# Moving gate rows to other engines and queues, and a weight preparation by one step, in a Mamba-style block on one core

## The chip, the cores and the metric

The kernel runs on one core of a Trainium2 chip. The metric is the device time of one execution in microseconds (us). A core has TensorE (PE; the profile lists its weight loads apart, as PEld), VectorE (DVE), ScalarE (ACT), GpSimd (POOL) and SyncE (SP), which here only issues DMAs. Each engine takes its own instructions strictly in the order of its queue; so does each engine's DMA issuing. A framework puts the instructions in order for every engine at build time, by the order of the program and by when it expects their inputs.

## The reference

For four sequences of 512 tokens with 512 features, the block computes

```python
mod = (silu(c) @ wmod).reshape(4, 6, 1, 512)      # sa, ca, ga, sb, cb, gb
ga = (2 * (ga >= 0) - 1) * maximum(abs(ga), 0.25) # gates; gb likewise
h = layernorm(x) * (1 + ca) + sa
x = x + ga * mamba2(h)                            # projection, conv, silu, chunked scan, output projection
h = layernorm(x) * (1 + cb) + sb
x = x + gb * (h @ binarized(weight).T + bias)
```

`binarized(w)` is the sign of each weight times the mean of the absolute values of its row. The Mamba part projects to x, B, C, z and dt, runs a causal convolution of four taps and SiLU over x, B and C, and then a scan in chunks of 128 tokens with 64 heads.

## The kernel before, in words

The 2,048 tokens are cut into eight halves of 256 tokens (`NHALF`, two to a sequence). Every half has two chunks, and every chunk four units of two head groups: 64 units in all. A unit takes one *step*. In a step `stage2` of unit s (the products `py`, L650, then gating by z) stands with `stage0` and `stage1` of unit s+2: `load_sums` (L535) fetches that unit's cumulated sums from DRAM (tile `decay`), `exps` (L544, line L549) takes 16 exponentials on ScalarE, and L625 multiplies them on VectorE by the masked product `gm`. The front part of half h+1 (norm, transposes `phT`, dt, projections and convolutions) is spread over the steps of half h by the list `SECOND` (`FRONT` for later halves); the tail of a chunk (`tail1`: the output projection `po`, L739, times the gates, L742; `tail2`: norm and transposes; `tail3`: the feed-forward product `pf`, L775) comes some steps after it. A table `steps`, filled by `at(step, f, ...)` from L814 on, holds all of this; within a step the functions are traced in the order in which they were entered.

What the change touches lies in steps 0 to 6, the first half's:

- `load_late` (step 0, L181) loads the modulation weights of the second, third, fourth and sixth part. They borrow tiles that are empty yet: `wout`, `bwT`, two z tiles and `room`, three rows of 512 per partition (L178), which later is the `gates` tile.
- `late_mods` (step 1, L233) multiplies them, copies the result to `rows` (L243; its tag `t` has one buffer, which the tail uses next), turns two of its parts into `modT`, and then makes the gate rows on the 64 partitions that hold them. VectorE does that in five instructions: twice the comparison with zero (L256), the absolute value as max(-g, g) (L257), the floor of 0.25 (L258), the product of sign and size (L259), and the second gate times the feed-forward bias `brow` (L260, 4 partitions). `brow` uses a buffer of tag `th`, `sg` and `ab` the two of tag `h2`. SyncE loads `brow` (L255) and writes the three rows to DRAM (`gate_d`, L262).
- `load_wout` (step 2, L265) loads the 2 MB output weights over the place of two modulation weights.
- `signs(o)` (steps 2 and 3, two of the four tiles each) loads a weight tile `fw` (L272, tag `h2`, two buffers, 256 KB), sums its absolute values (`alpha`, L274), makes its signs (`sw`, L277) and scales them on ScalarE (L278). `sw` lies in a buffer of tag `C` or `B`, three each, which also hold B and C of the halves.
- `turned_signs(o)` (steps 5 and 6) turns a tile on TensorE (L285) and copies it into `bwT` (L286), which `tail3` reads from step 7 on.
- `load_gates` (step 3, L719) broadcasts a sequence's rows from `gate_d` to all partitions; `tail1` reads them in step 4. `load_res` (L726) loads the residual `xr` in step 3.

`f_norm` of half 1 is also in step 1: statistics and L297 on VectorE, the root (`rs_a`, L298) on GpSimd, the normalisation (L300) on VectorE, then the transposes `phT` (L330). `f_dt` (step 2) is a chain of some 20 small VectorE instructions (L371 to L404), with four small DMA writes issued by GpSimd for all halves but the first (L389, L393, L407). A convolution (`conv_pair`, L440) starts on ScalarE (L450), takes three VectorE instructions (L454), which read the projection's PSUM tile, and ends with L459. PSUM tiles of tag `mm` have five buffers, and TensorE waits where the next product finds none.

Of the kernel before, what the change touches and what calls it, by code (L numbers as in the profile page):

```python
# [11 lines left out]
F32 = mybir.dt.float32  # L12
AF = mybir.ActivationFunctionType
ALU = mybir.AluOpType
# [4 lines left out]
B, L, DM = 4, 512, 512  # L19
# [21 lines left out]
def adaln_mamba_block(  # L41
# [15 lines left out]
    nc = tc.nc  # L57
# [13 lines left out]
    wk = ctx.enter_context(tc.tile_pool(name="wk", bufs=2))  # L71
# [47 lines left out]
    gate_d = dram.tile([B, 3, DM], F32, name="gate_d")  # L119
# [25 lines left out]
    def load_wm_at(t6, place, k0=0):  # L145

        n = place.shape[1]
        nc.sync.dma_start(place, wm_v[:, k0 : k0 + n, t6 * DM : (t6 + 1) * DM])
        for k in range(n):
            wms[t6, k0 + k] = place[:, k]  # L150
# [27 lines left out]
    room = wk.tile([P, 3, DM], F32, tag="gates", name="wm3_g", bufs=1)  # L178
    room_z = wm_tiles(3, "z", 6, 2)

    def load_late(h):  # L181

        load_wm_at(2, wout[:, 0:NK])
        load_wm_at(5, wout[:, NK:])
        load_wm_at(4, bwT)
        for k in range(2):
            load_wm_at(3, room_z[k].unsqueeze(1), k)
        load_wm_at(3, room[:, 0:2, :], 2)


    sc = keep.tile([P, NK, 32], F32, name="sc")
# [17 lines left out]
    def glued(products, after=None):  # L209

        with tc.issue_after(after) if after else nullcontext():
            first = products[0]()  # L212
        with tc.issue_after(first.ins), tc.high_priority(offset=1000):
            for product in products[1:]:
                product()  # L215
# [17 lines left out]
    def late_mods(h):  # L233

        pg = ps.tile([P, DM], F32, tag="mm", name="pg")
        glued([
            partial(
                mm, pg[32 * j : 32 * j + 32, :], sc[:, k, :], wms[t6, k], start=(k == 0), stop=(k == NK - 1)
            )
            for k in range(NK) for j, t6 in enumerate((2, 5, 4, 3))  # L240
        ])
        row = wk.tile([P, DM], F32, tag="t", name="rows", bufs=1)
        nc.vector.tensor_copy(row, pg)  # L243
        pm = ps.tile([P, NK, P], F32, tag="mm", name="pm")
        for dt in range(NK):
            nc.tensor.transpose(pm[:, dt, :], row[:, dt * P : (dt + 1) * P], ident)
        nc.vector.tensor_copy(modT[:, 2], pm[:, :, 96 : 96 + B])
        nc.vector.tensor_scalar(modT[:, 3], pm[:, :, 64 : 64 + B], 1.0, None, ALU.add)

        g = row[0:64, :]  # L250
        sg = wk.tile([64, DM], F32, tag="h2", name="sg")
        ab = wk.tile([64, DM], F32, tag="h2", name="ab")
        brow = wk.tile([64, DM], F32, tag="th", name="brow")
        second = slice(32, 32 + B)
        nc.sync.dma_start(brow[second, :], ffn_b.partition_broadcast(B))  # L255
        nc.vector.tensor_scalar(sg, g, 0.0, 2.0, ALU.is_ge, ALU.mult)  # L256
        nc.vector.scalar_tensor_tensor(ab, g, -1.0, g, ALU.mult, ALU.max)  # L257
        nc.vector.tensor_scalar(ab, ab, 0.25, None, ALU.max)  # L258
        nc.vector.scalar_tensor_tensor(sg, sg, -1.0, ab, ALU.add, ALU.mult)  # L259
        nc.vector.tensor_mul(ab[second, :], sg[second, :], brow[second, :])  # L260
        for i, v in enumerate((sg[0:B, :], sg[second, :], ab[second, :])):
            nc.sync.dma_start(gate_d[:, i, :], v)  # L262

    def load_wout():
        nc.sync.dma_start(wout, w_outT.rearrange("(k p) e -> p k e", p=P))  # L265
# [548 lines left out]
    def at(step, f, *args):  # L814
        steps.setdefault(step, []).append((f, args))

    for h in range(NHALF):
        for step, f, args in (FIRST, SECOND)[h] if h < 2 else FRONT:
            at(max(0, h - 1) * NU + step, f, h, *args)
        if h % HPB == 0:  # L820
            at(h * NU + 3, load_gates, h // HPB)
        if h == 0:
            at(0, load_late, h)
            at(1, behind, 0, late_mods)
            at(2, load_wout)
            for o in range(NK):
                at(o // 2 + 2, signs, o)
    for o in range(NK):
        at(o // 2 + 5, behind, 1, turned_signs, o)
    for h in range(NHALF):  # L830
# [9 lines left out]
    h = NHALF - 1  # L840
# [65 lines left out]
```

## Time and profile before

| | |
|---|---|
| median of three runs | 736.62 us (733.73 to 736.94) |
| the profiled execution's own time | 737.38 us |
| its span in the profile | 735.7 us |
| TensorE busy | 700.4 us (95%) |
| VectorE busy | 599.5 us (81%) |
| ScalarE busy | 522.0 us (71%) |
| GpSimd busy | 254.8 us (35%) |
| mean granted TensorE clock | 0.993 |

The profile is one execution. Its page cuts the span into 40 slices of 18.4 us and gives the busy share of each engine in tenths; PEclk is the clock that TensorE was granted, DMA the mean busy share of the 16 DMA engines. The chain of work that ended last is followed back from the last instruction, at each step to what released it. A line such as `PE a <- DVE b: 7.3, 2, 5.4` in the view of waits says that a on TensorE waited for b on VectorE 7.3 us in all, twice, at the longest 5.4. In the view of instructions over time a row has its start, its length (of several merged ones, from the first's start to the last's end), engine, line, operation, output and inputs, shapes and count, and in brackets how long the engine was idle before it and what ended that. SPq, DVEq and so on are the engines' queues, where DMAs are issued.

### The profile page before, as it was taken

How to read it: one execution, taken by the hardware profiler on the slowest of the kernel's cores; microseconds unless marked ns; L12 is line 12 of the kernel's file. 1: busy time of each engine (PE TensorE's matmuls, PEld its weight loads, DVE VectorE, ACT ScalarE, POOL GpSimd, SP SyncE). 2: the span in 40 equal slices, each digit the busy share in tenths (PEclk: the TensorE clock that was granted, in tenths of full speed). 3: DMA queues.
4: the chain of work that ended last, by engine and by line, in shares of the span. 5: the costliest groups of instructions: out<-in, count | busy, mean ns of one | idle time of the engine just before them, and what ended most of it. 6: DMA issues, size and time to landing. Idle time of an engine off the chain costs nothing.

```text
span 735.7 us, 15007 instructions
## 1 busy us (share of the span) xinstructions
PE 700.4 (95%) x5196; PEld 500.8 (68%) x5196; DVE 599.5 (81%) x1170; ACT 522.0 (71%) x1507; POOL 254.8 (35%) x297
## 2 busy tenths in 40 slices
PE   6999979899999999999999999999999999999997
PEld 3786746666677666677677666776667866677754
DVE  3869888876998678986899768996799867996995
ACT  2467658748696697785976787865968768788941
POOL 4021323444243332343223342433414332333652
PEclk9999989999999999999999999999999999999999
DMA  8991693535555256444644256552564537457720
GB/s 279 328 291 41 204 208 85 135 98 142 127 132 144 63 155 137 102 115 102 159 116 130 53 116 168 142 137 53 140 132 114 130 86 176 116 150 151 142 69 29
DMA packets 119067, 99.24 MB, mean 135 GB/s; under 512 B 73984, under 2 KB 97152, under 8 KB 118992
## 3 DMA queue, kind: packets, MB, share of 16 engines
q1 hardware_dynamic: 117808, 96.39, 52.3%
q0 software_dynamic: 896, 1.38, 0.7%
q8 instruction: 41, 0.67, 0.4%
q10 hardware_dynamic: 288, 0.52, 0.2%
q14 instruction: 34, 0.28, 0.1%
HBM read 92.47 MB, written 5.79 MB: 134 GB/s over the span
## 4 chain that ended last, share of the span: by engine, by line
PE 65%; ACT 16%; DVE 9%; DMA 4%; issue 4%; POOL 1%; SPq 1%; ACTq 0%; DVEq 0%; POOLq 0%
PE po L739 14%; PE pp_x L434 11%; PE pp_z L434 10%; ACT decay L549 9%; PE pp_C L434 7%; PE pp_B L434 5%; PE pf L775 3%; PE py L212 2%; PE py L215 2%; DVE decay L625 2%; ACT h L759 2%; DVE u_x L454 2%; DMA fw<-in_ffn_w 2%; ACT win L549 2%; PE gy L215 2%
## 5 line engine op out<-in xcount | busy, mean ns | idle before, releaser
L549 ACT ACTIVATE decay<-decay,st 128x128 f32<-128x128 f32 x960 | 293.9, 395 | 4.2 <-DMA decay<-sums_d 3.7
L625 DVE SCALAR_TENSOR_TENSOR decay<-decay,gm 128x1024 f32<-128x1024 f32 x120 | 160.8, 1341 | 50.3 <-ACT decay L549 47.2
L434 PE MATMUL pp_x<-hT,win 128*128 128x259 f32 x512 | 120.7, 390 | 7.3 <-DVE u_C L454 7.3
L434 PE MATMUL pp_z<-hT,win 128*128 128x256 f32 x512 | 118.1, 383 | 0.0
L434 PEld LDWEIGHTS pp_x<-hT,win 128*128 128x128 f32 x512 | 96.9, 193 | 25.2 <-ACT decay L549 7.7
L739 PE MATMUL po<-wout,z 128*128 128x512 f32 x256 | 113.8, 595 | 0.0
L434 PEld LDWEIGHTS pp_z<-hT,win 128*128 128x128 f32 x512 | 94.3, 189 | 16.3 <-issue 3.5
L675 POOL TENSOR_TENSOR z<-yt,z 128x256 f32<-128x256 f32 x62 | 62.9, 1015 | 76.1 <-DVE yt L674 57.8
L454 DVE SCALAR_TENSOR_TENSOR u_x<-pp_x,cw,u_x 128x256 f32<-128x256 f32 x192 | 83.6, 474 | 1.3 <-ACT u_x L450 0.7
L739 PEld LDWEIGHTS po<-wout,z 128*128 128x128 f32 x256 | 47.5, 190 | 53.1 <-issue 52.4
L672 POOL TENSOR_TENSOR yt<-yt,xs 128x256 f32<-128x256 f32 x46 | 41.4, 899 | 106.3 <-DVE yt L671 78.6
L507 POOL TENSOR_TENSOR xs<-u_x,rr 128x512 f32<-128x512 f32 x32 | 42.7, 1334 | 79.2 <-DVE u_x L459 61.3
L516 ACT ACTIVATE uz<-pp_z,zb 128x256 f32<-128x256 f32 x64 | 27.5, 470 | 59.0 <-PE pp_z L434 59.0
L215 PE MATMUL py<-decay,xpad 128*32 128x128 f32 x1680 | 66.3, 276 | 0.0
L434 PE MATMUL pp_B<-hT,win 128*128 128x259 f32 x256 | 63.5, 396 | 2.7 <-ACT decay L549 1.9
L434 PE MATMUL pp_C<-hT,win 128*128 128x259 f32 x256 | 59.6, 384 | 1.1 <-DVE u_x L454 1.1
L775 PE MATMUL pf<-bwT,h 128*128 128x512 f32 (+1 forms) x136 | 59.0, 578 | 1.4 <-ACT h L759 1.3
L434 PEld LDWEIGHTS pp_B<-hT,win 128*128 128x128 f32 x256 | 47.4, 193 | 14.5 <-ACT decay L549 3.1
L450 ACT ACTIVATE u_x<-pp_x,cb,cw 128x256 f32<-128x256 f32 x64 | 35.3, 560 | 30.5 <-PE pp_x L434 30.4
L434 PEld LDWEIGHTS pp_C<-hT,win 128*128 128x128 f32 x256 | 47.8, 189 | 9.4 <-PE pn L424 1.4
L679 POOL TENSOR_TENSOR xd<-xpad,st 128x256 f32<-128x256 f32 x48 | 34.1, 727 | 55.8 <-PE pst L215 28.3
L212 PE MATMUL py<-decay,xpad 128*32 128x128 f32 x240 | 47.4, 279 | 3.2 <-issue 2.2
(157 smaller groups left out, 1080.9 us busy)
## 6 DMA issues: line engine op xcount, KB each, us to landing
decay<-sums_d SPq DMA_DIRECT2D x120, 256.0 KB
decay<-sums_d SPq DMA_DIRECT2D x120, 128.0 KB
rr<-r_d SPq DMA_DIRECT2D x64, 128.0 KB
e<-e_d SPq DMA_DIRECT2D x96, 64.0 KB
win<-in_w_inT SPq DMA_DIRECT2D x4, 1024.0 KB
xr<-in_x SPq DMA_DIRECT2D x16, 256.0 KB
res<-o SPq DMA_DIRECT2D x15, 256.0 KB
x<-in_x SPq DMA_DIRECT2D x14, 256.0 KB
```

What stands on the lines that cost most here:

```text
L212: first = products[0]()
L215: product()
L434: last = mm(pm, win[:, k, col : col + P], H[h]["hT"][:, k, lo:], start=(k == 0), stop=(k == NK - 1))
L450: nc.scalar.activation(u[:, j, :], pm[:, KS - 1 :], AF.Identity, bias=cb[:, t : t + 1], scale=cw[:, t, KS - 1 : KS])
L454: nc.vector.scalar_tensor_tensor(u[:, j, :], pm[:, k : k + T], cw[:, t, k : k + 1], u[:, j, :], ALU.mult, ALU.add)
L507: nc.gpsimd.tensor_tensor(xs, xc, rr, ALU.mult)
L549: nc.scalar.activation(ets[r][:, i, :], ets[r][:, i, :], AF.Exp, bias=H[h]["st"][:, hd : hd + 1], scale=-1.0)
L625: nc.vector.scalar_tensor_tensor(ets[r], ets[r], 1.0, bc_mid(gm[:, r, :], HPG), ALU.min, ALU.mult)
L672: ew.tensor_add(t, t, xs)
L675: ew.tensor_mul(zg, t, zg)
L739: last_po = mm(po, H[h]["z"][g // 2][:, g % 2, c * CH : (c + 1) * CH], wout[:, g, :], start=(g == 0), stop=(g == NKI - 1))
L775: mm(pf, h2[:, k, :], bwT[:, k, cols], start=(k == 0), stop=(k == NK - 1))
```

## The change

The gate rows leave `late_mods` for a function `late_gates`, called in step 2 after `load_wout`. The comparison stays on VectorE (now giving plus or minus one half), the absolute value goes to ScalarE, the floor (now with a doubling) and the two products go to GpSimd, and the three writes of `gate_d` go to GpSimd's queue. `sg`, `ab` and `brow` lie in the three rows of `room`, not in buffers of `h2` and `th`; `brow` is loaded at the end of `load_late`, in step 0. `signs` comes one step later for every tile (steps 3 and 4); `turned_signs` stays in steps 5 and 6.

```diff
@@ load_late
         load_wm_at(3, room[:, 0:2, :], 2)
+        nc.sync.dma_start(brow[second, :], ffn_b.partition_broadcast(B))
@@ late_mods
-        g = row[0:64, :]
-        sg = wk.tile([64, DM], F32, tag="h2", name="sg")
-        ab = wk.tile([64, DM], F32, tag="h2", name="ab")
-        brow = wk.tile([64, DM], F32, tag="th", name="brow")
-        second = slice(32, 32 + B)
-        nc.sync.dma_start(brow[second, :], ffn_b.partition_broadcast(B))
-        nc.vector.tensor_scalar(sg, g, 0.0, 2.0, ALU.is_ge, ALU.mult)
-        nc.vector.scalar_tensor_tensor(ab, g, -1.0, g, ALU.mult, ALU.max)
-        nc.vector.tensor_scalar(ab, ab, 0.25, None, ALU.max)
-        nc.vector.scalar_tensor_tensor(sg, sg, -1.0, ab, ALU.add, ALU.mult)
-        nc.vector.tensor_mul(ab[second, :], sg[second, :], brow[second, :])
+        late_row.append(row)
+
+    late_row = []
+    second = slice(32, 32 + B)
+    brow = room[0:64, 2, :]
+
+    def late_gates(h):
+        g = late_row.pop()[0:64, :]
+        sg, ab = room[0:64, 0, :], room[0:64, 1, :]
+        nc.vector.tensor_scalar(sg, g, 0.0, 0.5, ALU.is_ge, ALU.subtract)
+        nc.scalar.activation(ab, g, AF.Abs)
+        nc.gpsimd.tensor_scalar(ab, ab, 0.25, 2.0, ALU.max, ALU.mult)
+        nc.gpsimd.tensor_tensor(sg, sg, ab, ALU.mult)
+        nc.gpsimd.tensor_tensor(ab[second, :], sg[second, :], brow[second, :], ALU.mult)
         for i, v in enumerate((sg[0:B, :], sg[second, :], ab[second, :])):
-            nc.sync.dma_start(gate_d[:, i, :], v)
+            nc.gpsimd.dma_start(gate_d[:, i, :], v)
@@ the table of steps
             at(2, load_wout)
+            at(2, late_gates, h)
             for o in range(NK):
-                at(o // 2 + 2, signs, o)
+                at(o // 2 + 3, signs, o)
```

## The prediction, made before the result was known

> **What bounds the kernel now.** I read the page's slices first: TensorE is 95% busy, and one slice is unlike the rest.
>
> ```profile
> PE   6999979899999999999999999999999999999997
> ...
> PEclk9999989999999999999999999999999999999999
> DMA  8991693535555256444644256552564537457720
> ```
>
> In the sixth slice (92 to 110 us) the clock that TensorE was granted falls, and before it DMA goes from empty to full. The waits between 64 and 150 us show TensorE's longest one there (total, times, longest):
>
> ```profile
> PE pp_x L434 <- DVE u_C L454: 7.3, 2, 5.4
> ```
>
> Stages of 3 us around it (columns: length, then PE, PEld, DVE, ACT, POOL busy with counts, clock, DMA share, GB/s):
>
> ```profile
> 91.00:94.00 3.00, 2.88 (x46) 1.99 (x44) 2.64 (x9) 1.58 (x4) 2.79 (x6) 1.00 1.16 198
> 94.00:97.00 3.00, 0.05 (x2) 0.00 (x0) 1.56 (x3) 1.09 (x2) 1.18 (x2) 1.00 1.09 230
> 97.00:100.00 3.00, 0.59 (x2) 0.53 (x3) 3.00 (x9) 2.48 (x8) 0.00 (x0) 0.61 1.03 279
> 100.00:103.00 3.00, 3.00 (x9) 2.33 (x8) 3.00 (x7) 1.10 (x3) 0.00 (x0) 0.50 1.07 260
> 103.00:106.00 3.00, 3.00 (x15) 2.33 (x13) 1.52 (x5) 2.71 (x9) 1.34 (x2) 0.75 1.05 181
> ```
>
> TensorE stands still for 5.4 us and then runs 6 us at a half to three quarters of its clock. The chain of that stretch (start, length, what) says why:
>
> ```profile
> 76.64 1.00 DVE ab L260
> ...
> 77.66 0.24 SPq L262
> ...
> 82.26 0.76 SPq L272
> ...
> 83.06 13.38 DMA fw<-in_ffn_w
> ...
> 96.46 0.69 DVE alpha L274
> ...
> 98.08 1.19 DVE u_C L454 x3
> ...
> 99.41 6.23 PE pp_x L434 x16
> ```
>
> The last gate row on VectorE (L260) holds SyncE's queue; behind it queue `wout` (2 MB) and the first two `fw` tiles; `fw` takes 13.38 us to land because DMA is full; VectorE's queue stands at `alpha` (L274), and the convolution of C, which must empty the PSUM tile that the next `pp_x` needs, is behind it. SyncE's own waits, and VectorE's queue:
>
> ```profile
> SPq L255 <- DVE u_x L459: 10.9, 1, 10.9
> ...
> SPq L262 <- DVE sg L259: 4.8, 1, 4.8
> SPq L262 <- DVE ab L260: 3.7, 1, 3.7
> ```
>
> ```profile
> 95.13 0.69 DVE L274 TENSOR_REDUCE alpha<-fw 128x1 f32<-128x512 f32 x1 [1.49 <-DMA fw<-in_ffn_w]
> 95.73 0.42 DVE L277 TENSOR_SCALAR sw<-fw 128x512 f32<-128x512 f32 x1
> 96.46 0.69 DVE L274 TENSOR_REDUCE alpha<-fw 128x1 f32<-128x512 f32 x1 [0.32 <-DMA fw<-in_ffn_w]
> 97.07 0.42 DVE L277 TENSOR_SCALAR sw<-fw 128x512 f32<-128x512 f32 x1
> ```
>
> SyncE stood 10.9 us before `brow` and 8.5 us before the gate rows' writes while DMA was nearly idle (share 0.07 from 64 to 76 us). After 125 us no single wait of TensorE is over 2.2 us, so what is won here stays won unless steps 3 to 6 give it back.
>
> **The change, part by part.** The sum is made against the profiled execution (737.38 us: span 735.7 and 1.7 around it); the median shown is 736.62, 0.8 less.
>
> *Gate rows off VectorE.* Removed: L256 0.42, L257 0.68, L258 0.41, L259 0.67, L260 0.99, start to start some 2.9 us. One comparison of L256's form returns (0.42). L256 to L258 stand right before `rs_a` (L297, 71.13), whose root on GpSimd releases the normalised x and so the transposes `phT`, before which TensorE waits 0.24 and 1.01 us. With `rs_a` some 1.3 us earlier those waits go; next late is TensorE itself, whose `pp_z` runs to 74.67. **-1.2 us.**
>
> *ScalarE's Abs.* It is between 0.27 (Abs 128x128, L372) and 0.59 us (copy 128x512, L223); I take 0.59, whose row has the same 512 columns. ScalarE idles 3.21 us before 74.71, which hides it; uncovered it would cost 0.59. L372 stands beside exponentials, and the trace has one table load in all, so none is added.
>
> *GpSimd's three operations and three DMA issues.* A product with 512 columns takes 1.28 (L745); two make 2.56. A one-input operation of this form isn't in the trace: between a 64x512 memset (0.66, L317) and the product (1.28); I take 1.0. The issues cost 0.53 to 0.77 each (L407, L393), 1.7 for three; a write lands after 1.8 to 1.9. In all 5.3 us of GpSimd, which idles 8.0 us before 85.10 and 4.0 before 90.66: hidden. Behind the gate rows on that queue stand the xs product and half 1's four DMA issues (90.66); if the 8.0 us gap weren't used, those would be up to 5.3 late, and what they write is read only some 25 us later. What it costs is VectorE's speed beside GpSimd: L459 takes 0.69 alone and 1.22 beside GpSimd's L675. Three GpSimd operations slow between none and three such instructions: 0 to +1.6; I take **+0.4**, as VectorE then runs mostly the short chain of f_dt.
>
> [...]
>
> *SyncE's queue.* `brow` moves to step 0, where its place in `room` is free. Gone are the 10.9 us before `brow` and the 4.8 and 3.7 before the gate writes. Behind them stood the third unit's decay sums, `rr`, `wout` and `fw`. `wout` waits for the last read of `wm2` and `wm5` (68.7) and can go about 10 us earlier, into idle DMA. Alone this is worth between 0 and 1.5 us (the third unit's exponentials come earlier, with ScalarE idle anyway); I take 0, but it makes the next term safer. The added wait: load_gates now follows GpSimd's writes. Behind it on SyncE stand `fw`, the residual `xr` and the fifth unit's sums; today it is issued at 95.12, and the writes should have landed near 88.
>
> *Signs one step later.* `alpha` and `sw` for o = 0, 1 leave the place before C's convolution. VectorE then goes from 93.6 straight to it; of the 5.36 us TensorE still waits for two or three convolution instructions, 0.9: **-4.5**. The first `pp_x` after it takes 6.23 us where others take 3.51 to 3.77: with the clock kept, **-2.5**. Intervals of 1 to 2 us elsewhere (before `phT`, for one) show no lower clock.
>
> [...]
>
> Given back: the four moved instructions (2.0 us start to start) land in 97 to 113, from which o = 2, 3's two reductions (1.27) go one step on. VectorE is busy 15.6 us from 94 to 113.8 today, 3.5 of them signs; with the new ones (2.2) that makes 14.3. From 92.4 (93.6 less the first term) it ends at 106.7, while TensorE, 8.2 earlier, would end `po` (113.8) at 105.6. That bounds the loss at 1.1 above and 0 below (VectorE idles 3 us there today); **+1.1**. In the next step VectorE sets the end (t, xr, the norm, 113.8 to 121.8), and two reductions are added: **+1.2**. `fw` shares buffers only with h2 now, so o = 0, 1 wait for no gate row; o = 2, 3 wait for their sw as before. The turning stays in steps 5 and 6, TensorE's work is the same. The sw tiles hold their B and C buffers one step less.
>
> Sum: -1.2 + 0.4 - 4.5 - 2.5 + 1.1 + 1.2 = **-5.5 us**: 731.9 against the profiled run, **731.1** against the median. Bounds: all gains, nothing back and the queue's 1.5: -9.7; gains halved and all given back: about 0.
>
> **Rivals.**
> 1. *The stall moves.* `alpha` waits for `fw` again, one step later, now in front of the tail's t and xr. For it: `fw` still queues behind load_gates and sums on SyncE, and a tile took 13.38 us to land. Against: `wout`, the bulk of the queue, should be gone. Then terms 2 and 3 come back as 7.0 elsewhere: -5.5 + 7.0 = +1.5, less up to 1.5 from the earlier sums: about 737.
> 2. *SyncE stands at load_gates.* If GpSimd takes the gate rows only behind f_dt's four issues, z and xd (to 95.2 today), they are written at 95.2 + 5.3 + 1.9 = 102.4, 7.3 us after today's 95.1. `fw`, xr and the fifth unit's sums then leave 7.3 late, VectorE stands at `alpha` in front of the tail, and the clock falls again (2.5): -5.5 + 7.3 + 2.5 = +4.3, **740.9**. It decides once the writes land more than some 4 us after SyncE gets there. Against it: the 8 us gap on GpSimd, and inputs ready at 69.7.
> 3. *The order is what counts and TensorE is full anyway:* the 5.4 us go, but VectorE, 87% busy from 64 to 150 us (75.1 of 86), gives nearly all back in steps 4 to 6; what stays is the 0.8 to 2.5 us by which its own work shrinks (2.9 less 0.4, less up to 1.7 for GpSimd): 734 to 736.
>
> **How the numbers follow.** My forecast (727 to 733) has 0.60; rivals 1 and 3 together 0.23; rival 2 0.17. Under 0.5% (3.7 us) a measurement can't tell from no change: faster 0.60, same 0.23, slower 0.17. The range takes in the bound below (727) and reaches through rivals 1 and 3 into rival 2's nearer half: 727 to 739.5. The forecast's own range is 727 to 733.
>
> **What would show it.** Right: SyncE issues `wout` near 70 us; no wait of TensorE over 2 us from 85 to 125; the granted clock stays at 1.0; the `pp_x` that took 6.23 takes under 4; load_gates waits little. Wrong: a wait of VectorE on `fw` before `alpha` in step 3 or 4 (rival 1); a long wait of SyncE on gate_d (rival 2); VectorE gapless to 150 us with TensorE waiting in small pieces (rival 3). The prediction fails altogether if the framework, which orders each engine's queue, reshuffles what comes after 125 us, which I take as unchanged.

## The result and the profile after

The changed kernel took **743.09 us** in the median of five runs (741.36 to 744.98), the kernel before 736.05 on the same chip: a ratio of 1.0105 (interval 1.0075 to 1.0135), 7 us slower where 5.5 us faster was forecast. The profiled execution's span is 741.4 us against 735.7, so the trace holds 5.7 us of the loss. Behind the change's own lines the line numbers are 9 higher than before (L434 is L443, L549 is L558). Units are counted from one here; the expectations for e1 to e5 count from zero where they call the unit with the exponentials around `hT` the third: it is the fourth.

From the page of the kernel after, the slices of TensorE's clock:

```profile
PEclk9999989899999999999999999999999999999999
```

The clock now falls twice, in the sixth slice as before (mean granted clock 0.82 from 92 to 111 us, before and after) and in the eighth (0.81 from 130 to 148 us). TensorE's waits from 60 to 160 us (total, times, longest):

```profile
PE pp_x L443 <- DVE u_C L463: 5.5, 1, 5.5
PE pp_x L443 <- ACT xpad L502: 4.4, 1, 4.4
PE pa L377 <- ACT hT L356: 2.5, 2, 1.3
```

The stall near 97 us, which was to go, is still there (5.36 before, 5.55 now). There is a new one of 4.4 us on ScalarE's copy `xpad`, and one of 2.5 us on `hT`. The starts of TensorE's products say where the time was lost: the first `po` starts 0.6 us earlier (106.62, now 106.02) but takes 7.72 us instead of 7.13 while the clock is still low (0.69 from 106 to 108 us, 1.00 before), and so ends level (113.75 and 113.74); the `pp_x` behind the new stall starts 4.3 us later (132.44, now 136.78); `pf` is 5.7 later (141.34, now 147.01), and so is everything after it. The whole loss thus arises between 114 and 147 us; the gains and losses ahead of it cancel. About 1.9 us of it are there before the new stall, in small waits of TensorE (the `py` in front of the stall starts at 129.43 before and at 131.31 now); the stall and the lower clock behind it (0.55 from 136 to 142 us) make the rest. The new stall in TensorE's queue:

```profile
136.78 6.01 PE L443 MATMUL pp_x<-hT,win 128*128 128x259 f32 x16 [4.38 <-ACT xpad L502]
```

The two stalls have different histories. The first, in VectorE's queue of the kernel after:

```profile
97.45 0.47 DVE L463 SCALAR_TENSOR_TENSOR u_C<-pp_C,cw,u_C 128x256 f32<-128x256 f32 x1
97.85 1.21 DVE L634 SCALAR_TENSOR_TENSOR decay<-decay,gm 128x1024 f32<-128x1024 f32 x1
98.98 0.67 DVE L283 TENSOR_REDUCE alpha<-fw 128x1 f32<-128x512 f32 x1
99.57 0.41 DVE L286 TENSOR_SCALAR sw<-fw 128x512 f32<-128x512 f32 x1
99.91 0.67 DVE L283 TENSOR_REDUCE alpha<-fw 128x1 f32<-128x512 f32 x1
100.50 0.41 DVE L286 TENSOR_SCALAR sw<-fw 128x512 f32<-128x512 f32 x1
100.83 0.47 DVE L463 SCALAR_TENSOR_TENSOR u_C<-pp_C,cw,u_C 128x256 f32<-128x256 f32 x1
```

`alpha` and `sw` of o = 0, 1, entered one step later, stand in front of the last instruction of C's convolution; before, they stood in front of its last four. The fifth unit's two decay products (L634, at 95.11 and 97.85) now stand in front of it too; before, they came behind it (101.53 and 106.22). No row has an idle time: VectorE waits for no `fw` any more, it is simply full from 94 to 106. The second stall is prepared on ScalarE. Busy time in stages of 6 us (the fourth pair of columns is ScalarE), first of before, then of after:

```profile
111.00:117.00 6.00, 6.00 (x47) 3.73 (x46) 4.48 (x9) 4.76 (x13) 0.00 (x0) 1.00 0.08 17
117.00:123.00 6.00, 5.22 (x63) 4.09 (x61) 5.58 (x10) 6.00 (x19) 4.11 (x4) 1.00 0.34 96
```

```profile
111.00:117.00 6.00, 6.00 (x61) 3.82 (x60) 3.96 (x9) 1.35 (x2) 0.00 (x0) 1.00 0.02 9
117.00:123.00 6.00, 4.84 (x56) 4.03 (x54) 4.61 (x11) 1.90 (x4) 4.50 (x5) 1.00 0.61 144
```

ScalarE worked 10.76 of these 12 us before, and 3.25 now. The first copy `xpad` in its queue before, and its queue after:

```profile
130.48 0.59 ACT L493 COPY xpad<-pt_xt 128x512 f32<-128x512 f32 x1
```

```profile
116.02 0.72 ACT L287 ACTIVATE sw<-sw,alpha 128x512 f32<-128x512 f32 x1 [4.26 <-DVE sw L286]
...
120.52 0.40 ACT L558 ACTIVATE decay<-decay,st 128x128 f32<-128x128 f32 x1
123.19 0.72 ACT L287 ACTIVATE sw<-sw,alpha 128x512 f32<-128x512 f32 x1 [2.27 <-DVE sw L286]
...
130.57 2.45 ACT L558 ACTIVATE decay<-decay,st 128x128 f32<-128x128 f32 x8
132.91 0.56 ACT L459 ACTIVATE u_C<-pp_C,cb,cw 128x256 f32<-128x256 f32 x1
133.35 2.45 ACT L558 ACTIVATE decay<-decay,st 128x128 f32<-128x128 f32 x8
135.69 0.56 ACT L459 ACTIVATE u_C<-pp_C,cb,cw 128x256 f32<-128x256 f32 x1
136.14 0.58 ACT L502 COPY xpad<-pt_xt 128x512 f32<-128x512 f32 x1
```

It idles, or waits for `sw`, and then the seventh and eighth units' exponentials stand in one block with the copies of C (`u_C`, 127.24 before, 132.91 now) and `xpad` (130.48 before, 136.14 now). TensorE waits for that copy. Why it idled: the sixth unit's exponentials, which ran at 112 to 118 before, now run at 102 to 108, as their sums come earlier; and the seventh's can't be had, since their tile is read by the fifth unit's `py`. Before, half of that `py` stood ahead of `po` in TensorE's queue (106.05); now all of it stands behind (114.75). The first rows of that `py`, before and after, and the row of SyncE's queue after that fetches those sums:

```profile
106.05 0.30 PE L212 MATMUL py<-decay,xpad 128*32 128x128 f32 x1
```

```profile
114.75 0.30 PE L213 MATMUL py<-decay,xpad 128*32 128x128 f32 x1
```

```profile
115.50 0.49 SPq L550 DMA_DIRECT2D decay<-sums_d  x1
```

### The profile page after: what moved, and what is told of

Read it like the earlier page. It is cut to its first block, busy times and chain, and to the rows that moved or that the text cites. A ratio compares the mean times of both kernels' runs of the same rounds, so it can differ in the third digit from the quotient of the medians.

```text
span 741.4 us, 15011 instructions
## 1 busy us (share of the span) xinstructions
PE 701.7 (95%) x5196; PEld 501.8 (68%) x5196; DVE 596.0 (80%) x1166; ACT 522.6 (70%) x1508; POOL 259.7 (35%) x303
## 4 chain that ended last, share of the span: by engine, by line
PE 61%; ACT 19%; DVE 12%; issue 4%; DMA 2%; POOL 1%; SPq 0%; ACTq 0%; POOLq 0%; DVEq 0%
PE po L748 13%; ACT decay L558 11%; PE pp_x L443 11%; PE pp_z L443 10%; PE pp_C L443 6%; PE pp_B L443 5%; PE pf L784 3%; DVE decay L634 3%; DVE u_x L463 2%; PE py L216 2%; PE py L213 2%; ACT h L768 2%; ACT win L558 2%; DMA decay<-sums_d 2%; PE gy L216 1%
## 5 line engine op out<-in xcount | busy, mean ns | idle before, releaser
L558 ACT ACTIVATE decay<-decay,st 128x128 f32<-128x128 f32 x960 | 294.0, 395 | 2.8 <-DMA decay<-sums_d 2.6
L634 DVE SCALAR_TENSOR_TENSOR decay<-decay,gm 128x1024 f32<-128x1024 f32 x120 | 160.9, 1342 | 55.0 <-ACT decay L558 53.1
L443 PE MATMUL pp_x<-hT,win 128*128 128x259 f32 x512 | 122.4, 394 | 9.9 <-DVE u_C L463 5.5
L443 PE MATMUL pp_z<-hT,win 128*128 128x256 f32 x512 | 118.1, 383 | 0.0
L443 PEld LDWEIGHTS pp_x<-hT,win 128*128 128x128 f32 x512 | 97.8, 195 | 28.1 <-issue 8.1
L443 PEld LDWEIGHTS pp_z<-hT,win 128*128 128x128 f32 x512 | 94.4, 189 | 16.2 <-issue 3.5
L443 PE MATMUL pp_B<-hT,win 128*128 128x259 f32 x256 | 62.6, 391 | 2.7 <-ACT decay L558 1.9
L443 PE MATMUL pp_C<-hT,win 128*128 128x259 f32 x256 | 59.6, 384 | 1.2 <-DVE u_x L463 1.2
L443 PEld LDWEIGHTS pp_B<-hT,win 128*128 128x128 f32 x256 | 46.5, 189 | 14.1 <-ACT decay L558 3.1
L443 PEld LDWEIGHTS pp_C<-hT,win 128*128 128x128 f32 x256 | 47.9, 190 | 9.1 <-PE pn L433 1.4
L688 POOL TENSOR_TENSOR xd<-xpad,st 128x256 f32<-128x256 f32 x48 | 35.1, 747 | 46.5 <-ACT xpad L502 24.9
```

The source lines that it names most:

```text
L443: last = mm(pm, win[:, k, col : col + P], H[h]["hT"][:, k, lo:], start=(k == 0), stop=(k == NK - 1))
L558: nc.scalar.activation(ets[r][:, i, :], ets[r][:, i, :], AF.Exp, bias=H[h]["st"][:, hd : hd + 1], scale=-1.0)
L634: nc.vector.scalar_tensor_tensor(ets[r], ets[r], 1.0, bc_mid(gm[:, r, :], HPG), ALU.min, ALU.mult)
```

## The experiments

Every kernel was timed against the kernel before on the same chip. The theories, in the order in which they were formed: T1, the later signs cost, by the C buffer that `sw` of o = 2 waits for; T2, the front costs, by Abs and by exponentials ahead of `hT`; T3, freeing SyncE's queue costs, by early sums; T4, the place of the fifth unit's `py` costs.

**e1 and e2: the two parts alone.** e1 has the gate rows' part, with `signs` in their old steps; e2 has only the later `signs`.

```diff
# e1, against the kernel after
-                at(o // 2 + 3, signs, o)
+                at(o // 2 + 2, signs, o)
# e2, against the kernel before
-                at(o // 2 + 2, signs, o)
+                at(o // 2 + 3, signs, o)
```

> The gate rows' part of the change alone; the signs stay in steps 2 and 3. Theory T1 (the loss comes from the signs' step: the sw tile of o = 2 gets its C buffer only when o = 0 has been turned in step 5, ScalarE stands before its scaling, and 16 exponentials behind it come late, so that TensorE stands 4.4 us near 132 us and loses its clock): this kernel lacks that stall and is 5 to 8 us faster than the changed kernel, 734 to 738. Theory T2 (the loss comes from the front: Abs stands on ScalarE's queue 2.7 us before the exponentials, and the third unit's exponentials, whose sums now come early, go between the four hT copies, so that the chain of f_dt starts 3.2 us late): it is as slow as the changed kernel, 741 to 744.

> The signs one step later alone; the gate rows stay on VectorE and SyncE's queue. T1: it has the stall near 132 us and loses 4 to 7 us against the kernel before, 740 to 743. T2: it is as fast as before or faster, and, with the alpha reductions gone from before C's convolution, TensorE's wait of 5.4 us near 94 us shrinks: 729 to 736.

e1: 740.82 us, ratio 1.0062 (1.0048 to 1.0076). e2: 732.65, ratio 0.9961 (0.9948 to 0.9974). The signs' part does what the prediction said in kind, at some two thirds of the size (-4.7 forecast, some -3 measured); the gate rows' part, which was put at -0.8 us, costs 4 to 5. Neither reproduces the stall of 4.4 us on `xpad`. Of the 6.8 us that e1's view puts on exponentials, 4.0 are the old stall's place (98.81) and 2.8 lie before the second `pp_x` (141.24); in both places an instruction of the convolution on VectorE ended within 0.1 us of the exponential, so which of the two released TensorE isn't told apart. The parts don't add: +0.62% and -0.39% make +0.23%, and the whole is +1.05%. TensorE's waits from 60 to 160 us, e1 and then e2:

```profile
PE pp_x L443 <- ACT decay L558: 6.8, 2, 4.0
```

```profile
PE pp_x L434 <- DVE u_C L454: 3.4, 2, 1.9
```

**e3 and e4: the turning earlier, and Abs on VectorE.** Both against the whole change.

```diff
# e3
-        at(o // 2 + 5, behind, 1, turned_signs, o)
+        at(o // 2 + 4, behind, 1, turned_signs, o)
# e4
-        nc.scalar.activation(ab, g, AF.Abs)
+        nc.vector.scalar_tensor_tensor(ab, g, -1.0, g, ALU.mult, ALU.max)
```

> The changed kernel with the turning also one step apart as before (steps 4 and 5 in place of 5 and 6), so that o = 0's buffer is free a step earlier. T1: the wait of ScalarE before the scaling of o = 2 goes, and with it the stall near 132 us: 735 to 738. T2: nothing changes in the front, 741 to 744.

> The changed kernel with the absolute value on VectorE (one instruction of 0.68 us, as before) and not on ScalarE. T1: within 1.5 us of the changed kernel, 741 to 744. T2: the 2.7 us before the exponentials go, hT and f_dt come 2 to 3 us earlier, and the time falls by 2 to 3, to 739 to 741.

e3: 736.36, ratio 1.0002 (0.9989 to 1.0014); the stall near 132 is gone, that near 97 stays at 5.5. e4: 743.83, ratio 1.0109 (1.0094 to 1.0124). Abs on ScalarE isn't the cause. e3 seemed to show that the C buffer, which keeps `sw` of o = 2 waiting until o = 0 is turned, is; but in its trace half of the fifth unit's `py` is ahead of `po` again (108.00, `po` 108.79), so it changed two things.

**e5 to e8: the front, and SyncE's queue alone.**

```diff
# e5, against e1; e7 has it too
-  (2, f_hT, ()), (2, f_dt, ()),
+  (1, f_hT, ()), (2, f_dt, ()),
# e6, against the kernel before; the added line ends load_late
+        nc.sync.dma_start(room[32 : 32 + B, 2, :], ffn_b.partition_broadcast(B))
-        brow = wk.tile([64, DM], F32, tag="th", name="brow")
+        brow = room[0:64, 2, :]
-        nc.sync.dma_start(brow[second, :], ffn_b.partition_broadcast(B))
# e7, against the kernel after: e3 and e5 together
# e8, against e2: e3's line
```

> The gate rows' part alone (as in e1: signs at their old steps), with f_hT of half 1 entered one step earlier, so that its copies of hT stand on ScalarE ahead of the third unit's 16 exponentials again. In e1 TensorE waited 2.5 us for hT, and the part alone cost 4.6 us (740.8 against 736.2). T3 (with SyncE's queue freed, the decay sums come early and exponentials stand on ScalarE in front of the copies that TensorE needs): the wait on hT is under 0.5 us, the chain of f_dt starts some 2.5 to 3 us earlier than in e1, and the time is 737 to 739; the rest of e1's loss, the waits of pp_x on the exponentials near 130 us (1.5 and 2.8), stays unless it follows from the front. Rival (the order in front is harmless, the loss is made near 130 us alone): the wait on hT goes, and the time stays at 740 to 741.5.

> The kernel before with one edit: the 4-partition load of brow goes to step 0 and to the third row of room; the gate rows stay on VectorE and on SyncE's queue, signs in their old steps. No compute instruction is added, removed or moved by the program; only SyncE's wait of 10.9 us ahead of brow goes, so that what is queued behind it comes earlier. T3: the earlier sums put exponentials ahead of copies on ScalarE, so the kernel becomes slower, by 1.5 to 4.5 us: 737.5 to 740.5. The rival, which is the prediction's own figure for SyncE's queue (0, at best -1.5): 734.5 to 736.2.

> The whole change, with the turning one step earlier (as in e3, 736.4) and f_hT of half 1 one step earlier (as in e5): both places where the runs so far show a wait that the change brought are undone. T3: TensorE's 2.5 us for hT go, the chain of f_dt and with it the convolution of C starts 2 to 3 us earlier, so the 5.5 us wait of pp_x for u_C near 97 us falls to 2 to 3 us, and with it the clock's fall: 731 to 734. Rival (VectorE is gapless from 94 us on and sets the end of that stage whatever comes ahead of it): 735.5 to 737.

> The kernel before with the signs one step later (as in e2, 732.7) and the turning one step earlier; gate rows as before. If the buffers of C that the signs hold cost time in e2 as they did in the whole change, this gives another 1 to 3 us: 730 to 731.5. If they only cost time where ScalarE's queue is filled with early exponentials (T3), there is nothing to win here: 732 to 734, TensorE's work of turning being only moved.

e5: 740.09, ratio 1.0063 (1.0043 to 1.0083). The wait on `hT` is gone and the ratio is e1's, as the rival said. Its profiled run doesn't show that what is won in front is lost again: there `po` starts 1.6 us before e1's (104.22, e1 105.83) and the span is 1.4 us shorter (737.6, e1 739.0), but the six runs spread from 738.8 to 743.6. e6: 735.44, ratio 1.0 (0.9991 to 1.0009). The sixth unit's exponentials come at 104.8, as in the slow kernels, and nothing is lost. But e6 frees SyncE's queue only in part. The wait before `brow` moves to the gate rows' writes, which VectorE still feeds (13.4 us there, 4.8 before); the third unit's sums are fetched at 73.00 (73.35 before, 63.42 in the whole change) and `wout` is issued at 77.36 (81.79 and 68.40). So T3 falls for what e6 frees; the whole freeing wasn't timed apart from the rest of the gate rows' part. e7: 733.19, ratio 0.9965 (0.9951 to 0.9979), the change itself with two edits, and faster than both kernels. e8: 736.08, ratio 0.9998 (0.9985 to 1.0011): the edit that wins 7 us in e3 loses 3 in e2, since the turning now stands ahead of `po` and TensorE waits there for `sw` (1.8 us in all), after a wait of `py` for exponentials (1.8, at 100.70).

**e9 to e12: the place of py.** In step 4 (index from zero) `tail1` of the first chunk is entered after `stage2`, so that the fifth unit's `py` comes ahead of `po`: in the whole change (e9), in e1 (e10), in the kernel before (e11) and in e2 (e12).

```diff
         for f, args in steps.get(step, []):
-            f(*args)
+            if (f, args) != (tail1, (0, 0)):
+                f(*args)
...
             stage2(*units[step])
+            if step == NP:
+                tail1(0, 0)
```

> The whole change, with one edit in step 4: the first chunk's output projection (tail1, po) is entered after stage2 of the fifth unit instead of ahead of it, so that py of that unit stands ahead of the 16 matmuls of po in TensorE's queue. In the kernel before, half of this py stood ahead of po (106.05) and freed one of two decay tiles, whose next sums were fetched at 107.41; in the whole change and in e1 all of it stands behind po (114.75, sums at 115.50), and ScalarE, which has nothing else to do, idles until the seventh unit's sums are there and then must run their exponentials in front of the copies that TensorE waits for at 132 us. T4 (the loss lies in the place of py in TensorE's queue): sums at 100 to 108, the exponentials of the seventh unit some 6 us earlier, the wait of pp_x near 132 gone or under 1.5, time 735 to 738.5 against 743.1. Rival T1 (only the C buffer that holds up sw of o = 2 counts): sw still comes at 122 or later, the stall at 132 stays, 741 to 744.

> The gate rows' part alone (e1, 740.8), with py of the fifth unit entered ahead of po as in e9. Signs are in their old steps, so no C buffer is late. T4: the place of py is what cost e1 its 4.6 us; the waits of pp_x on exponentials near 130 us (6.8 in all in e1) fall under 2, time 734 to 737. Rival (e1 loses at the front, by exponentials ahead of hT, and by the earlier sums): 739 to 741.

> The control: the kernel before with py of the fifth unit entered ahead of po; half of it stood there already. If the edit of e9 and e10 only mends what the change broke (T4), this changes little: 734 to 737. If having all of py ahead of po is a gain in itself, which would also explain a gain in e9 and e10 without T4, it is as large here: 731 to 733.

> The signs' part alone (e2, 732.7, the fastest so far), where py stands wholly behind po too, with py of the fifth unit entered ahead of po. In e2 ScalarE had 16 exponentials of its own to run during po (109.8 to 114.5) and the seventh unit's started at 118.2, so by T4 its place costs little there: 731 to 733. If it costs as in e1 (some 3 us or more): 728 to 730.5.

e9: 735.01, ratio 0.9987 (0.9971 to 1.0004), 8 us less than the whole change. e11: 736.3, ratio 1.0013 (0.9997 to 1.0029), and e12: 733.19, ratio 0.9968 (0.9956 to 0.9981): by itself the edit is worth nothing. e10: 738.06, ratio 1.004 (1.0025 to 1.0056): a part of e1's loss (1.0062) goes; the median lies between what T4 and what the rival said. ScalarE's and SyncE's queues in e9:

```profile
114.18 4.77 ACT L558 ACTIVATE decay<-decay,st 128x128 f32<-128x128 f32 x16
...
121.63 0.72 ACT L287 ACTIVATE sw<-sw,alpha 128x512 f32<-128x512 f32 x1
```

```profile
109.15 0.49 SPq L550 DMA_DIRECT2D decay<-sums_d  x1
```

The sums are fetched 6.35 us earlier than in the whole change (a little later than expected), all 16 exponentials of the seventh unit run in ScalarE's empty time, and the stall near 132 is gone. `sw` of o = 2 is as late as ever (121.63 against 123.19), but the exponentials are ahead of it. So it isn't the late `sw` by itself that costs, but that in the whole change the exponentials had to come behind it. The gate rows' part still costs something with `py` ahead: e10 lies 1.8 us over e11, and e9 as much over e12, which have the same edit without that part.

**e13 to e16: py behind in the kernel before; signs behind the convolution.** e13 forces the fifth unit's `stage2` behind `po`. e14 enters `signs` in the same steps of the whole change, but after `f_C` and `f_x`; e15 adds e9's edit, e16 also e5's.

```diff
# e13, against the kernel before; first_po[0] is the last matmul of the first po
-            stage2(*units[step])
+            if step == NP:
+                with tc.issue_after(first_po[0].ins):
+                    stage2(*units[step])
+            else:
+                stage2(*units[step])
# e14, against the kernel after: moved behind the loop that enters FIRST, SECOND and FRONT
-            for o in range(NK):
-                at(o // 2 + 3, signs, o)
...
     for o in range(NK):
+        at(o // 2 + 3, signs, o)
+    for o in range(NK):
         at(o // 2 + 5, behind, 1, turned_signs, o)
```

> The kernel before with stage2 of the fifth unit (its py) forced behind the last matmul of po, where the whole change has it; nothing else. T4 in its strong form (the place alone is the loss): a stall of TensorE near 130 us as in the whole change, 739 to 743. T4 in its weak form (the place costs only where the sums, and with them the sixth unit's exponentials, come early, so that ScalarE has nothing to do during po; in the kernel before it runs 16 of them at 112 to 118): 735.5 to 738.

> The whole change with signs entered in the same steps, but behind f_C and f_x (step 3) and f_x (step 4) instead of ahead of them, so that alpha and sw of o = 0, 1 stand behind C's convolution in VectorE's queue. If the order within the step kept the wait of pp_x on u_C (5.5 us at 97): it falls to 3.5 or less (the four instructions are 1.9 us), and the clock's fall with it, 2 to 4 us in all before po; the stall near 132 stays, since py is still behind po: 738 to 741.5. If the late f_dt chain (exponentials ahead of hT) and the early decay products keep it: the wait stays over 4.5, and 741.5 to 744.

> e14's edit and e9's (py ahead of po) in the whole change: both stalls mended. By the first reading of e14: e9's 735.0 less 2 to 4, 731 to 733. By the second: 734 to 735.5.

> e15 with hT of half 1 entered one step earlier as well (e5's edit), so that TensorE doesn't wait 2.5 us for hT near 77 and the f_dt chain starts earlier. e7 gained 3 us by it over e3. Expected 728.5 to 731.5, the fastest so far (the prediction's 731.1 within it); if it gives nothing in this place, as in e5 against e1: 731 to 733 like e15.

e13: 736.82, ratio 1.0012 (1.0 to 1.0025): the place of `py` alone costs at most 2 us in the kernel before. e14: 742.07, ratio 1.0074 (1.0055 to 1.0092), by its time the second reading. TensorE's waits in it:

```profile
PE pp_x L443 <- ACT xpad L502: 5.4, 2, 2.9
PE pp_x L443 <- DVE u_C L463: 4.0, 2, 3.7
```

The wait at 97 falls from 5.55 to 3.70, by just the 1.85 us of the four instructions (98.98 to 100.83), so in the whole change the order within the step is what kept them there; the wait lies between what the two readings said. The waits on `xpad` are still there, twice. e15: 742.22, ratio 1.008 (1.0052 to 1.0109): a miss. Both mends are in, and the time is lost in a third place: `ph` of the tail waits 4.8 us, since in its trace two `sw`, one `alpha` and two decay products stand ahead of and between the tail's instructions on VectorE (115 to 126 us), and `pp_C` comes after 7 us in which TensorE works some 2 (128.18, 5.87 us long instead of 3.77). e16: 735.55, ratio 0.9989 (0.9977 to 1.0), short of the expected 731; it waits 3.5 us at the same `ph`.

**e17: both conditions, built from the kernel before.** e6's and e13's edits together.

> The kernel before with e6's edit (brow loaded in step 0, 735.4 by itself) and e13's (py of the fifth unit behind po, 736.8 by itself). If the loss of the whole change is the meeting of early exponentials and a late py: the sixth unit's exponentials at 103 to 107, ScalarE busy less than 5 of the 12 us from 111 to 123 (before 10.8, whole change 3.3), waits of pp_x on ScalarE or on what it feeds between 128 and 142, and 739 to 744. If the two effects only add (or the moved work itself is needed): 735 to 737.5.

e17: 735.71, ratio 1.0008 (0.9992 to 1.0023). ScalarE is emptier from 111 to 123 (6.87 us busy of 12), though not under the 5 us that were expected, and nothing is lost: `py` runs at 111.37 there, not at 114.75, the seventh unit's exponentials start at 117.61, and both `u_C` copies (126.94) stand ahead of the eighth unit's. So the two conditions, as far as e17 brings them about, don't make the loss by themselves; it frees SyncE's queue no more than e6 does.

All kernels in one table (times in us; "traced" is the time of the profiled run, to which the columns left of it belong; the second `xpad` copy is the one next to the last `pp_x` ahead of `pf`):

| kernel | sixth unit's exponentials | fifth unit's py | second xpad | traced | median |
|---|---|---|---|---|---|
| e2 | 109.8 | behind po, 110.2 | 133.16 | 733.4 | 732.7 |
| e12 | 105.7 | behind 2 of po's 16 | 132.91 | 732.9 | 733.2 |
| e7 | 106.3 | ahead | 133.87 | 733.3 | 733.2 |
| e9 | 102.8 | ahead | 135.46 | 735.1 | 735.0 |
| e6 | 104.8 | half ahead | 135.78 | 735.1 | 735.4 |
| e16 | 104.1 | behind 6 of po's 16 | 135.61 | 735.2 | 735.6 |
| e17 | 104.8 | behind, 111.4 | 137.70 | 735.0 | 735.7 |
| before | 112.2 | half ahead | 138.46 | 737.4 | 736.1 |
| e8 | 108.1 | ahead | 136.87 | 737.0 | 736.1 |
| e11 | 109.6 | half ahead | 138.40 | 736.3 | 736.3 |
| e3 | 101.4 | half ahead | 135.03 | 735.1 | 736.4 |
| e13 | 113.4 | behind, 114.8 | 140.55 | 739.1 | 736.8 |
| e10 | 106.4 | behind 2 of po's 16 | 138.54 | 738.7 | 738.1 |
| e5 | 104.6 | behind, 112.4 | 139.52 | 739.3 | 740.1 |
| e1 | 105.9 | behind, 114.0 | 140.97 | 740.7 | 740.8 |
| e14 | 104.3 | behind, 112.1 | 141.03 | 739.6 | 742.1 |
| e15 | 106.8 | behind 6 of po's 16 | 141.74 | 741.8 | 742.2 |
| after | 102.1 | behind, 114.8 | 144.06 | 743.1 | 743.1 |
| e4 | 104.1 | behind, 116.4 | 145.71 | 744.4 | 743.8 |

Five of the six over 740 (e15 is slow for the other reason above) have both early exponentials and `py` at 112 or later. That line was drawn after the fact, and e17 lies only 0.7 us on its other side. The profiled runs of e13 (2.3 us over its median) and e14 (2.4 under) don't stand for the median.

## Why the prediction was wrong

**The step that failed** is the assumption, named at the end as the one that would make all fail and given neither a price nor a chance, that the order after 125 us stays; the order changes from 76 us on. On the unchanged order rested the gate rows' part: -1.2 and +0.4 with "SyncE's queue" taken as 0, as "the third unit's exponentials come earlier, with ScalarE idle anyway", so -0.8 in all. That part alone (e1) costs some 4.6 us, and in the whole change TensorE stands 4.38 us for ScalarE's copy at 132 to 137 us and then runs `pp_x` in 6.01 us, where others take 3.67 to 3.77. Freed, SyncE brings the sums and `wout` earlier (`wout` is issued at 68.40, before at 81.79; `fw`, one step later by the change, at 89.27, before at 82.26). The queues of three engines are then ordered otherwise. ScalarE has the fourth unit's 16 exponentials between the `hT` copies (from 76 to 82 us it is busy 6.00 of 6 us, before 3.55); VectorE has the fifth and sixth units' decay products early; TensorE has `py` wholly behind `po`. The whole change's loss needs the last of these: with `py` ahead, 8 us are won back (e9). Whether the freed queue by itself is worth 0 stays open: e6, which frees a part of it, costs nothing (ratio 1.0), and with `py` ahead the whole gate rows' part still costs some 2 us (e10 against e11, e9 against e12).

The other part, the later signs, was right in its mechanism and too large in its sum: -4.5, -2.5, +1.1 and +1.2 make -4.7, and e2 gains some 3. The parts were added, and they don't add.

Point by point:

- *Gate rows off VectorE, -1.2:* right where it was looked for. The waits before `phT` are gone, and `phT` ends 2.6 us earlier (77.65, now 75.07; 0.8 of it is from the stretch ahead). But `hT` comes behind the exponentials, and the chain of f_dt starts 3.2 us later (its first `dl`: 80.58, now 83.78).
- *Abs, hidden:* 0.63 us as estimated (0.59), but not hidden where the prediction put it: it waits 2.72 us for the rows with the third unit's 16 exponentials behind it, which start at 69.31 instead of 66.72. e4, without it, is no faster than the whole change, so it costs nothing that lasts.
- *GpSimd:* 1.94, 1.27 and 2.13 us and 1.84 for the three issues, 7.2 instead of 5.3. Still hidden: the rows are issued by 78.7, and `load_gates` goes at 88.74 with no long wait. Rival 2 fell. Of VectorE's speed beside it, +0.4: the decay product at 74.11 and L531 at 75.83 take 1.69 and 1.64 us instead of 1.23 and 0.69, some 1.4 more and near the upper bound of 1.6; VectorE then idles 1.15 us, so this isn't where the time was lost.
- *Stall, -4.5, and clock, -2.5:* the mechanism is right, as e2 shows by itself: the wait falls from 5.36 to 1.91 (-3.45), `pp_x` takes 5.43 instead of 6.23 (-0.8, as the clock falls after this rest too, to 0.57 from 97 to 100 us), and the first `po` ends 4.6 us earlier. In the whole change the wait is 0.2 longer, since "VectorE then goes from 93.6 straight to it" is false there: `signs` are entered ahead of `f_C` in the step and four of their instructions are placed in front of its end (1.85 us, e14). Being entered ahead isn't enough for that: in e2 and e7 they are entered ahead too and stand behind it (`alpha` at 105.12 and 100.16). The wait is 2.87 in e7 and e16, where `hT` comes earlier, against 3.70 in e14.
- *Given back, +1.1 and +1.2:* in e2 nothing is up to there: `po` ends 4.6 us earlier, and the third `po` starts 4.5 earlier (154.35, then 149.82); its span is 4.0 shorter. The 15.6 us that VectorE was said to be busy from 94 to 113.8 are 15.1 in the profile, so the bound of 1.1 would have been 0.6.
- *"o = 2, 3 wait for their sw as before":* wrong. `sw` of o = 2 waits until o = 0 is turned and holds ScalarE's queue 2.27 us at 123.19, with the seventh unit's exponentials behind it. Where these are ahead of it (e9), it costs nothing.
- *Rivals:* none of the three came, nor does any reach 743. Rival 3's picture of a gapless VectorE holds from 94 to 106 us; its time (734 to 736) doesn't.

**What is settled:** the whole change loses its time where TensorE waits for ScalarE's copies between 127 and 147 us, most of it at the stall near 132 us with its lower clock (0.55), since these copies stand behind exponentials that came late; this comes from the order of the queues and is undone by e3 or e9, with the moved work left as it is. Abs, GpSimd's work, the late `sw` by itself, the sums as early as e6 has them, and the place of `py` in the kernel before are not enough to make it. **What stays open:** which condition beyond the two of e17 makes e1, e5 and e14 slow (the full freeing of SyncE's queue is a candidate that wasn't timed alone); and why the framework's order changes as it does, which no trace shows. Giving the sw tiles buffers of their own wasn't tried.

## What to carry to other kernels

Where a program orders the queues at build time, an edit that makes an input arrive earlier need not be free where "the engine idles anyway": ask what is put ahead of what on every engine that receives it, and compare the order of the queues before trusting a sum of local gains. Parts of such a change don't add, so time them apart: here the later signs alone are the gain (732.65), and the change needed two edits of order to get the same (e7, 733.19). When an engine idles for several microseconds although the work of the next unit exists, look for the buffer that work waits for, and for who reads it last.

## What the runs showed of the hardware

- **A rest of 1.9 us can cost clock, and need not.** In e2 TensorE stood still for 1.91 us (94.25 to 96.16), the granted clock fell to 0.57 from 97 to 100 us, and `pp_x` took 5.43 us instead of 3.77. In e8 it stood still for the same 1.91 us before the same `pp_x`, which took 3.75 (rows of e2 and e8 below). After 1.91 us in e12 the same product took 5.42, and after 1.85 in e6 `pp_C` took 5.33, where the one at 122.96 in the kernel before took 3.96. After 1.93 in the kernel before (132.44) `pp_x` took 3.75 at a clock of 1.00 (132 to 138 us), and after 1.93 in e2 (118.86) the clock was 1.00 too (117 to 123 us). So the length of the rest alone doesn't decide, and no run shows what does. After 2.87 us (e7) eight matmuls took 3.65 us instead of 2.00 (clock 0.77 from 97 to 100 us and 0.66 from 100 to 103), after 3.70 us (e14) 3.44 (0.94 and 0.50 in the same stretches). A rest of 1.0 us before `phT` in the kernel before (76.67) cost none: the clock was 1.00 from 76 to 82 us.

```profile
96.16 5.43 PE L434 MATMUL pp_x<-hT,win 128*128 128x259 f32 x16 [1.91 <-DVE u_C L454]
```

```profile
94.67 3.75 PE L434 MATMUL pp_x<-hT,win 128*128 128x259 f32 x16 [1.91 <-DVE u_C L454]
```

- **GpSimd's work on 4 partitions wasn't cheaper here than on 64.** A product on 4 partitions of 512 took 2.13 us where one on 64 took 1.27, and the one-input `tensor_scalar` on 64 took 1.94 (the estimate was 1.0). VectorE was busy beside the first, so whether that lengthened it isn't told apart. VectorE's decay product (L634) took 1.63 instead of 1.21 us at 95.11, beside `xd` products (L688) and DMA issues of GpSimd, and 1.23 at 71.78, beside one such product.
